# One rotation of banks for two passes, factors of the q weights loaded early, one border memset per pair of stages, and the relu of k ahead of the widening

## The chip, the cores and the metric

The kernel runs on one core of one Trainium2 chip. The metric is device time in microseconds (us), taken as the median over several executions. PE is the matrix engine (TensorE), DVE the vector engine, ACT the scalar engine, POOL is GpSimd and SP is the engine whose queue issues all of this kernel's DMAs. A time such as "1958.7" is a place on the time axis of the one profiled execution, counted from the start of its span.

## The reference

Two layers follow each other on x of shape (8, 256, 64, 64), in float32.

```
# layer 0: attention with reduced keys
xr  = layernorm_over_channels(conv(x, w_sr, stride 4))      # 16 x 16 places
q   = w_q x ;  k, v = split(w_kv xr)                         # 8 heads of 32
x   = x + gamma_s * w_out( softmax(q k^T / sqrt(32)) v )
# layer 1: linear attention at two scales
qkv = w_qkv x                                                # 768 channels
dw  = depthwise_conv_5x5(qkv, w_dw)
agg = grouped 1x1 conv of dw (w_pw, 96 groups of 8)
ms  = concat(qkv, agg)                                       # 64 heads of 8
q, k = relu(q), relu(k);  v = [v, 1]
out = q (k^T v);  out = out[:-1] / (out[-1] + 1e-15)
x   = x + batchnorm(w_proj out)
```

## The kernel before

The work is done in three passes over all images. The **first pass** (`first_pass`, 0 to about 1928 us) does layer 0 and the product by `w_qkv`. Its loop counts 128 steps `n`, one for half of a strip of an image. In a step PE makes scores (L849), their product with v (L881) and the output product (L949), and then some products of `qkv` (L996). `qkv` of an image's group `g` (four groups an image, so 32 in all) is made with seven products in place of eight for each of three pairs of outputs; DVE and ACT combine the seven from PSUM. The pairs are made in the order 1 (k), 2 (v), 0 (q). Pairs 0 and 1 go to DRAM scratch as planes with a border of zeros (`stage`, L1009), through two tiles `stage0` and `stage1` with one buffer each. The border is written by POOL with `memset`, in `new_stages` (L972), for each pair anew: pair 1 in step n+1, pair 0 in step n+3. Pairs 1 and 2 also go out as tokens through transposed tiles (`turned`, L1016). At the end of the pass two numbers that say whether the softmax sums stayed in bounds are reduced on DVE, summed with one matmul (`total`, L1195), and compared (L1197 to L1200).

The **second pass** (`second_pass`, about 1928 to 2966 us) loops over 64 units `u`, one for each (t, k, b): two halves t, four groups of channels k, eight images b. For one unit it loads the grids `d`, the tokens `kq` and `vq` (eight DMAs, `load_tokens` L1281), makes the depthwise and grouped convolution together as matmuls over widened weights `w` (L1389 in `convolve`, and L1420 in `product`, which does two units of q at once), the sums of k by v for the plain scale (`raw`, L1458) and for the convolved one (`sums`, L1483), and counts (L1470, ones by a sum over tokens of k that POOL makes: `red_raw` and `red_agg`, L1366 to L1368). DVE and POOL make differences of the grids first (`c`, L1310 and L1312, and `y`, L1338 and L1339). ACT takes the relu of the loaded k (`positive`, L1373) and of the convolved one (`r`). The weights are widened from small factors `wd` and `ws` (`factors`, L570), by ACT (L592, L615), DVE and POOL (L603); these are `chores`, of which `do(n)` takes the next n. A unit with image 1 or 2 is "wide": it takes 13 chores at the place where others take 4.

The **third pass** (about 2807, interleaved with the end of the second, to 3525 us) loads the kv sums (`kvp`, `kvq`, L1742 and L1744, summed by DVE at L1754 and L1755 and spread at L1758 and L1764), and per part of an image the denominators (`den`, L1816), their reciprocal, its spread over channels (`rep`, L1834), the product with q by DVE (L1839) and the projection (`p`, L1850).

Instructions are put in order on each engine by a scheduler with a cost model, except where `keep_in_program_order` (called `pinned` in the second pass) holds them in the order of the program text. The tile framework adds the waits. A tile pool's memory that is taken over by a later pool waits for the last readers of what was there before. Both passes make their own PSUM pools: the first rotates through eight banks with a list `turns`, the second has a pool each for `cv` (6 banks), `raw` and `sums` (1 each). So the first matmul of the second pass waits for all banks of the first:

```
psums = {
    tag: ctx.enter_context(tc.tile_pool(name=f"psum_{tag}", bufs=1, space=bass.MemoryType.PSUM))
    for tag in ("cv", "raw", "sums")
}
```

The end of a unit's step in the second pass, where the relu and the chores lie, is:

```
        products(u, 1)
        ...
        do(13 if wide else 4)
        if now:
            summed_raw(u)
        ...
        if u + 1 < n_all:
            positive(u + 1)
            reduced_raw(u + 1)
```

Of the kernel before, what the change touches and what calls it, by code (L numbers as in the profile page):

```python
# [32 lines left out]
P = 128  # L33
# [536 lines left out]
def factors(nc, home, a, j, k, n):  # L570


    wd = home.tile([P, 4, n, R * R], F32, tag=f"wd_{n}", name=f"wd_{j}_{k}")
    ws = home.tile([P, 4, D1], F32, tag=f"ws_{n}", name=f"ws_{j}_{k}")
    nc.sync.dma_start(wd[:, :, :4], a.w_big[:, j, 4 * k : 4 * k + 4].rearrange("p g (n f) -> p g n f", n=4))
    nc.sync.dma_start(ws, a.w_small[:, j, 4 * k : 4 * k + 4])
    across = wd[:, :, n - (2 if n == 6 else 3) :][:, :, :2]
    nc.vector.tensor_add(across, wd[:, :, 0:4:2], wd[:, :, 1:4:2])
    if n == 9:
        nc.vector.tensor_add(wd[:, :, 4], wd[:, :, 1], wd[:, :, 3])  # L580
        nc.vector.tensor_add(wd[:, :, 5], wd[:, :, 0], wd[:, :, 2])
        nc.vector.tensor_add(wd[:, :, 8], wd[:, :, 6], wd[:, :, 7])
    return wd, ws
# [45 lines left out]
def first_pass(ctx: ExitStack, tc: tile.TileContext, a, fine, planes, x2d, kd, vd, ready):  # L629
# [12 lines left out]
    psum = ctx.enter_context(tc.tile_pool(name="psum", bufs=1, space=bass.MemoryType.PSUM))  # L642
    turns, kept = list(range(8)), {}
# [12 lines left out]
    def load(src, name):  # L656
        consts[name] = const.tile(list(src.shape), F32, tag=name, name=name)
        nc.sync.dma_start(consts[name], src)
# [313 lines left out]
    def new_stages(b, g, pair):  # L972
        for j in (2 * pair, 2 * pair + 1):
            st = rest.tile([P, 4, NB + 1, NB + 1], F32, tag=f"stage{j % 2}", name=f"stage_{b}_{g}_{j}", bufs=1)
            tc.keep_in_program_order(nc.gpsimd.memset(st[:, :, 0 if g // 2 else NB], 0.0))
            tc.keep_in_program_order(nc.gpsimd.memset(st[:, :, :, 0 if g % 2 else NB], 0.0))
            staged[b, g, j] = st
# [3 lines left out]
    def qkv(b, g, pair):  # L981
# [5 lines left out]
        stages = [staged.pop((b, g, j)) for j in js] if pair < 2 else None  # L987
# [71 lines left out]
        def p1():  # L1059
            ps = product(1, w[:, 0, 0], b11)  # L1060
            u[1] = part(1)
            nc.scalar.copy(u[1], ps)  # L1062
# [28 lines left out]


# [33 lines left out]
    for n in range(n_all + 6):  # L1126
        now, was = n < n_all, 0 <= n - 1 < n_all
        at = n % 16
        filled = now and n // 16 + 1 < B
        if filled and at == 5 and n > 16:  # L1130
            load_x(n // 16 + 1)
        if filled and at == 5:
            ahead = keys_values(n // 16 + 1)
            next(ahead)
        if now and at == (10 if n < 16 else 1):
            border(n // 16)

        if now:
            e0 = scores(*order[n], 0, q[n])
            ej[n] = joined(*order[n], e0)  # L1140
        if (n, 0) in blank:
            new_stages(*blank.pop((n, 0)), 0)
        catch_up(late)
        if was:
            p = order[n - 1]
            for kc in range(2):
                valued(*p, kc, es[n - 1][kc])
            counted(*p, ej.pop(n - 1))
            es.pop(n - 1)
            copied(*p)  # L1150
            normed(*p)
        if now:
            es[n] = e0, scores(*order[n], 1, q.pop(n))
            joined_too(ej[n], es[n][1])
        catch_up(later)
        if (n, 1) in blank:
            new_stages(*blank.pop((n, 1)), 1)

        products = todo.pop(n, [])
        taps = 2 if filled and 6 <= at < 10 else 0  # L1160
        for f in products[:3]:
            f()
        if filled and at >= 10:
            next(ahead, None)
        for _ in range(taps):
            next(ahead)
        if 0 < n + 1 < n_all:
            if n + 1 not in q:
                q[n + 1] = queries(*order[n + 1])
        for f in products[3:]:  # L1170
            f()
        if was and p[2]:
            b, s = p[:2]
            pair = [att[b, s, 0], att[b, s, 1]]
            for oc in range(2):
                added(b, s, pair, oc)
            if s % 2:
                differences(b, s // 2)
                blank[n + 1, 1] = blank[n + 3, 0] = b, s // 2
                rest_of = [f for pair in (1, 2, 0) for f in qkv_lazy(b, s // 2, pair)]  # L1180
                for i, count in enumerate((7, 4, 7, 3)):
                    todo[n + 1 + i] = rest_of[:count]
                    rest_of = rest_of[count:]
        for _ in range(taps):
            next(ahead)
        if filled and at >= 10:
            next(ahead, None)
        if now and n >= n_all - 40:
            next(ready, None)


    both = halves.tile([P, 2], F32, tag="both", name="both")
    nc.vector.tensor_reduce(both, seen.rearrange("p (n k) -> p k n", k=2), AX.X, ALU.add)
    total = bank("total")[:, :2]
    nc.tensor.matmul(total, mean_w, both, start=True, stop=True)  # L1195
    fits = halves.tile([P, 4], F32, tag="fits", name="fits")
    nc.vector.tensor_scalar(fits[:, 0:1], total[:, 0:1], SUM_MAX / D0 / C, None, ALU.is_le)  # L1197
    nc.vector.tensor_scalar(fits[:, 1:2], total[:, 1:2], INVERSE_MAX / D0 / C, None, ALU.is_le)
    nc.vector.tensor_mul(fits[:, 2:3], fits[:, 0:1], fits[:, 1:2])
    nc.vector.tensor_copy(fine, fits[:, 2:3])  # L1200

# [8 lines left out]
def second_pass(ctx: ExitStack, tc: tile.TileContext, a, planes, kd, vd, kept, first_w, kvd, kvg, qd, ahead):  # L1215
    nc = tc.nc
    B = a.x.shape[0]
    def pool(name, bufs=1):
# [4 lines left out]
    late, quads, between, const, small, third, w_q = (  # L1223
        pool("late2"), pool("quads2"), pool("between2", 2), pool("const2"), pool("small2", 2), pool("third2"),
        pool("wq2"),
    )
    soon = ExitStack()
    second, even, first, odd, extra, w_taps, pairs, sides, mid = (
        soon.enter_context(tc.tile_pool(name=name, bufs=bufs))
        for name, bufs in (  # L1230
            ("second2", 1), ("even2", 1), ("first2", 1), ("odd2", 1), ("extra2", 1), ("taps2", 1), ("pairs2", 1), ("sides2", 2),
# [3 lines left out]
    psums = {  # L1235
        tag: ctx.enter_context(tc.tile_pool(name=f"psum_{tag}", bufs=1, space=bass.MemoryType.PSUM))
        for tag in ("cv", "raw", "sums")
    }

    pinned = tc.keep_in_program_order  # L1240

    def bank(tag, name, bufs=1, n=512):
        return psums[tag].tile([P, n], F32, tag=tag, name=name, bufs=bufs)

    units = [(t, k, b) for t in range(2) for k in range(4) for b in range(B)]
# [57 lines left out]
    def paired(u, i):  # L1303
        d = grids[u]
        c = cells[u, i] = pairs.tile([P, 4, (NB + 1) * NB // 2], F32, tag=f"c1_{i}", name=f"c1_{u}_{i}")
        v = c.rearrange("p g (y x) -> p g y x", x=NB // 2)
        d0, d1, d2 = (d[:, :, :, i : i + NB - 1 : 2] for i in range(3))
        if i == 2:

            pinned(nc.gpsimd.tensor_copy(v, d1))  # L1310
        else:
            nc.vector.tensor_sub(v, d2 if i else d0, d1)  # L1312
# [68 lines left out]
    def convolve(u, i):  # L1381
        t, k, b = units[u]
        c, w = cells[u, i], wt[t, k]
        ps = bank("cv", f"cv1_{u}_{i}", 6)
        for g in range(4):
            for da in range(2):
                n = 2 * da + i if i < 2 else 4 + da
                cols = slice(da * (NB // 2), da * (NB // 2) + P)
                nc.tensor.matmul(  # L1389
# [6 lines left out]
        if i == 2:  # L1396
            both = between.tile([P, QB], F32, tag="both", name=f"both1_{u}")
            nc.scalar.copy(both, ps)
            r = (second if u % 2 else sides).tile([P, 2, 4, P], F32, tag="r1", name=f"r1_{u}", bufs=1)
# [9 lines left out]
    def product(m, i, j):  # L1409
        t, k, b = units[2 * m]  # L1410
        now, w = quad[m], wq[t, k, (i, j)]
        ps = bank("cv", f"cv0_{m}_{i}{j}", 6)
        for g in range(4):
# [6 lines left out]
            nc.tensor.matmul(out, w[:, g], x, start=True, stop=True)  # L1420
# [31 lines left out]
    def summed_raw(u):  # L1452
        kq, vq = kqs.pop(u), vqs[u]
        ps = bank("raw", f"raw_{u}")
        for i in range(8):
            r, c = i // 4, i % 4
            for f in range(4):
                nc.tensor.matmul(  # L1458
# [8 lines left out]
    def counted(ps, at, red):  # L1467
        for j in range(4):
            cols = slice(j * D0, (j + 1) * D0)
            nc.tensor.matmul(ps[cols, at : at + 1], red[:, cols], ones, start=True, stop=True)  # L1470
# [5 lines left out]
    def summed(u):  # L1476
# [3 lines left out]
        for i in range(8):  # L1480
            par, r, c = i // 4, i // 2 % 2, i % 2
            for h in range(4):
                nc.tensor.matmul(  # L1483
# [23 lines left out]
    def ended_raw(u):  # L1507
# [3 lines left out]
        mraws[u] = m  # L1511

# [34 lines left out]
    def load_factors(u, what):  # L1547
        t, k, b = units[u]
        j = t + 2 * what
        parts[j, k] = factors(nc, kept if what else w_q, a, j, k, 6 if what else 9)  # L1550

    def spare(name):
        return bank("cv", name, 6)

    load_factors(0, 0)
# [3 lines left out]
    reduced_raw(0)  # L1559
    for u in range(n_all + 3):  # L1560
# [21 lines left out]
        if u < 2:  # L1582
            chores.append(weights_q(0, u))
# [14 lines left out]
        do(3 if wide else 2)  # L1598
# [7 lines left out]
        do(3 if wide else 2)  # L1606
# [8 lines left out]
        if u in (n_all - 1, n_all + 1):  # L1615
            ahead.send(spare)
        do(13 if wide else 4)
# [8 lines left out]
        if u + 1 < n_all:  # L1626
            positive(u + 1)
# [28 lines left out]
def third_pass(ctx: ExitStack, tc: tile.TileContext, a, planes, x2d, kvd, kvg, qd, out, kept, top):  # L1656
# [119 lines left out]
    def folded(b, get=None):  # L1776
        dw, kt = folds[b]
        wp = homes["mid"].tile([P, 4, C], F32, tag="wp", name=f"wp_{b}") if b else first_wp
# [216 lines left out]
def kernel_body(ctx: ExitStack, tc: tile.TileContext, a, out):  # L1995
# [22 lines left out]
    with ExitStack() as held:  # L2018
        kept = held.enter_context(tc.tile_pool(name="kept", bufs=1))
        first_w = kept.tile([P, 4, 6 * P], F32, tag="w1_0", name="w1_0_0")  # L2020

        def ready():
            yield from widened_k(tc, first_w, *factors(nc, kept, a, 2, 0, 6))

        first_pass(tc, a, fine, planes, x2d, kd, vd, ready())
        top = held.enter_context(tc.tile_pool(name="top3", bufs=1, side="right"))
        ahead = third_pass(held, tc, a, planes, x2d, kvd, kvg, qd, out, kept, top)
        second_pass(tc, a, planes, kd, vd, kept, first_w, kvd, kvg, qd, ahead)
# [125 lines left out]
```

## Time and profile before

| | us |
|---|---|
| median of 3 runs (from, to) | 3544.17 (3543.93, 3544.29) |
| the profiled execution, its time | 3526.67 |
| its span | 3524.9 |
| PE busy | 3449.2 (98%) |
| DVE busy | 2251.0 (64%) |
| POOL busy | 1844.9 (52%) |
| ACT busy | 1473.7 (42%) |

The span is the time from the first to the last instruction that the profiler saw; the execution's own time is 1.8 us longer. The mean granted clock of PE is 0.99 of full speed. A line of a timeline shows the start, the duration, the engine, the line of the code, the operation with what it writes and reads, how many of them lie together, and, in brackets, the idle time ahead of it on its engine with the instruction or transfer that ended it. In the list of waits a line shows who waited for whom: in all, how often, and the longest.

### The profile page before, as it was taken

Reading aid. Unit: us, or ns where it says so; the run is one execution under the profiler, and the core shown is the slowest. Engines: PE = TensorE matmul, PEld = TensorE weight load, DVE = VectorE, ACT = ScalarE, POOL = GpSimd, SP = SyncE. Lnnn points to the kernel's source line nnn. Section 1 sums busy time; section 2 is a strip of 40 time slices with the busy share of each in tenths; the row PEclk is TensorE's granted clock in tenths of the full one; section 3 lists DMA queues with packets and bytes.
Section 4 is the critical chain, followed back from the end, with each engine's and each line's share of the span. In section 5 each row is a group of like instructions: output and inputs, shape, how many; then the busy total and the mean of one; then the engine's idle time right before and its main releaser. Section 6 shows DMA issues by size and latency. Waiting matters only on the chain.

```text
span 3524.9 us, 92777 instructions
## 1 busy us (share of the span) xinstructions
PE 3449.2 (98%) x38818; PEld 2105.2 (60%) x38818; DVE 2251.0 (64%) x3441; ACT 1473.7 (42%) x3385; POOL 1844.9 (52%) x1756
## 2 busy tenths in 40 slices
PE   8999999999999999999999899999999999999998
PEld 5554555555546555455444788888888874333343
DVE  1567476576675765766777677777777774544443
ACT  2345354353453544544553444444444332333332
POOL 3557466465564664655664555666656642222221
PEclk9999999999999999999999999999999998999999
DMA  5445446355364463553555999999999978787872
GB/s 175 115 108 159 122 112 173 96 163 147 89 172 118 102 188 93 148 154 92 141 134 149 268 262 272 266 268 269 274 268 266 274 209 253 232 237 228 242 220 88
DMA packets 577196, 647.36 MB, mean 184 GB/s; under 512 B 81664, under 2 KB 452864, under 8 KB 576768
## 3 DMA queue, kind: packets, MB, share of 16 engines
q1 hardware_dynamic: 576768, 641.34, 65.0%
q8 instruction: 307, 5.03, 0.6%
q14 instruction: 121, 0.99, 0.1%
HBM read 389.85 MB, written 249.23 MB: 181 GB/s over the span
## 4 chain that ended last, share of the span: by engine, by line
PE 90%; DMA 4%; SPq 2%; ACT 1%; POOL 1%; DVE 1%; issue 1%; DVEq 0%; POOLq 0%; ACTq 0%
PE qkv L996 17%; PE p L1850 11%; PE cv L1389 9%; PE sc L849 8%; PE av L881 7%; PE cv L1420 7%; PE sums L1483 6%; PE o L949 6%; PE q L831 6%; PE sr L752 6%; PE av L907 2%; PE rep L1834 2%; PE den L1816 1%; PE raw L1458 1%; DMA raw<-planes 1%
## 5 line engine op out<-in xcount | busy, mean ns | idle before, releaser
L862 ACT ACTIVATE e<-sc 128x512 f32<-128x512 f32 x1024 | 528.6, 603 | 508.4 <-PE sc L849 508.4
L901 POOL TENSOR_TENSOR ef<-ef,e 128x512 f32<-128x512 f32 x512 | 688.3, 1354 | 91.1 <-ACT e L862 67.5
L894 POOL TENSOR_TENSOR ef<-e 128x512 f32<-128x512 f32 x256 | 329.6, 1307 | 545.8 <-ACT e L862 545.7
L1389 PE MATMUL cv<-w,c 128*128 128x128 f32 x3072 | 386.5, 280 | 5.9 <-DVE stage L1009 4.2
L1860 POOL TENSOR_TENSOR y<-z,xs 128x512 f32<-128x512 f32 x120 | 156.1, 1303 | 445.5 <-ACT z L1858 382.2
L1389 PEld LDWEIGHTS cv<-w,c 128*128 128x128 f32 x3072 | 363.4, 194 | 7.7 <-POOL c L1310 4.7
L849 PE MATMUL sc<-q,kk 32*64 32x256 f32 x8192 | 298.5, 387 | 5.6 <-ACT e L862 5.2
L996 PE MATMUL qkv<-differences,combined 128*128 128x512 f32 x576 | 289.2, 593 | 0.4 <-POOL differences L966 0.4
L928 DVE STREAM_TRANSPOSE rden<-av 128x256 f32<-128x256 f32 x256 | 99.7, 427 | 283.6 <-ACT att L919 236.1
L1483 PE MATMUL sums<-vq,r 128*32 128x288 f32 x4096 | 265.6, 407 | 0.2
L1858 ACT ACTIVATE z<-p,held 128x512 f32<-128x512 f32 x128 | 99.5, 777 | 374.6 <-PE p L1850 368.5
L849 PEld LDWEIGHTS sc<-q,kk 32*64 32x64 f32 x8192 | 155.3, 131 | 163.0 <-issue 101.4
L881 PE MATMUL av<-e,vv 64*32 64x256 f32 x8192 | 252.3, 379 | 0.0
L752 PE MATMUL sr<-x,wsr 128*128 128x256 f32 x1024 | 236.1, 383 | 8.0 <-DMA wsr<-in_w_sr_dram 7.7
L831 PE MATMUL q<-x,wq 128*128 128x512 f32 x512 | 241.9, 594 | 0.0
L1366 POOL TENSOR_TENSOR red_raw<-kq 128x512 f32<-128x512 f32 x64 | 82.1, 1282 | 298.7 <-ACT kq L1373 239.7
L752 PEld LDWEIGHTS sr<-x,wsr 128*128 128x128 f32 x1024 | 194.8, 191 | 64.5 <-issue 31.6
L949 PE MATMUL o<-att,wout 128*128 128x512 f32 x512 | 230.3, 592 | 0.0
L934 DVE TENSOR_TENSOR att<-att,rall 128x512 f32<-128x512 f32 x128 | 217.3, 1698 | 4.4
L1850 PE MATMUL p<-raw,wp 128*128 128x512 f32 x448 | 215.7, 603 | 1.8 <-ACT wp L1785 1.8
L1012 DVE TENSOR_TENSOR whole<-part,qkv 128x512 f32<-128x512 f32 x256 | 172.2, 682 | 66.6 <-ACT part L1062 49.4
L1420 PE MATMUL cv<-y,w 128*128 128x128 f32 x1536 | 200.6, 277 | 10.2 <-POOL y L1339 7.2
(174 smaller groups left out, 6058.8 us busy)
## 6 DMA issues: line engine op xcount, KB each, us to landing
planes<-stage SPq DMA_DIRECT2D x128, 578.0 KB
d<-planes SPq DMA_DIRECT2D x128, 578.0 KB
vq<-v SPq DMA_DIRECT2D x256, 256.0 KB
raw<-planes SPq DMA_DIRECT2D x64, 578.0 KB
x<-in_xp_dram SPq DMA_DIRECT2D x64, 512.0 KB
wsr<-in_w_sr_dram SPq DMA_DIRECT2D x128, 256.0 KB
x<-x SPq DMA_DIRECT2D x128, 256.0 KB
k<-turned SPq DMA_DIRECT2D x256, 128.0 KB
```

What stands on the lines that cost most here:

```text
L752: nc.tensor.matmul(ps[:, oc], w[:, ci, oc * P : (oc + 1) * P], strips(b, f // 2)[:, ci, f % 2 * NK : (f % 2 + 1) * NK], start=(f == ci == ...
L831: nc.tensor.matmul(ps, consts["wq"][:, ci, c * P : (c + 1) * P], strips(b, s)[:, ci], start=(ci == 0), stop=(ci == 1),)
L849: nc.tensor.matmul(scs[h][HALVES[half], QH[kq % 2]], kks[b][rows, c, kq * P // 2 : (kq + 1) * P // 2], qs[rows, QH[half]], start=True, sto ...
L862: nc.scalar.activation(e[:, h % 2].rearrange("p q n -> p (q n)"), scs[h], AF.Exp, scale=D0**-0.5)
L881: nc.tensor.matmul(sums["av"][half][cols, : QB // 2], vvs[b][rows, kq, c * P + h * D0 : c * P + (h + 1) * D0], es[h // 2][rows, h % 2, kq ...
L901: tc.keep_in_program_order(nc.gpsimd.tensor_tensor(f, f, e[:, :, half], ALU.add))
L949: nc.tensor.matmul(ps, consts["wout"][:, c, oc * P : (oc + 1) * P], att[c], start=(c == 0), stop=(c == 1))
L996: nc.tensor.matmul(ps, w, x, start=True, stop=True)
L1389: nc.tensor.matmul(ps[:, g * P : (g + 1) * P], c[:, g, cols], w[:, g, n * P : (n + 1) * P], start=(da == 0), stop=(da == 1),)
L1420: nc.tensor.matmul(out, w[:, g], x, start=True, stop=True)
L1483: nc.tensor.matmul(ps[h * D0 : (h + 1) * D0, : 36 * D1].rearrange("p (r n e) -> p r n e", r=3, e=D1), kt[:, par, h, 2 * r + c], vq[:, r : ...
L1850: nc.tensor.matmul(as_block(ps, i // 2), wp[:, i, oc * P : (oc + 1) * P], block(g, i // 2, i % 2, j), start=(i == 0), stop=(i == 3),)
```

## The change

The change has these parts.

1. One PSUM pool with eight banks serves both passes; the second pass takes bank 2 for `raw`, bank 6 for `sums` and the others for `cv`. The matmuls of the second pass are pinned until the raw sums of three units are through.
2. The factors of the first q weights (`wd`, `ws`, with nine sets each) are loaded in the first pass, into the memory of the weights for k and v (`wkv`), and summed there. 18 of the q weights' chores are done ahead of unit 0, and units' first two `do` are empty for u = 0. The scheduler also puts vq_0's eight loads into the first pass.
3. `new_stages` is called once for both pairs, in step n+1.
4. `positive(u + 1)` comes ahead of `do(13 if wide else 4)`.
5. `total` and the comparisons move into step n_all + 2 of the first pass. For units 0 and 1 the copy of c_2 is ACT's in place of POOL's.
6. Some tiles change pools: `const2`, `r1` of odd units, and `wp` of odd images. With this the scheduler issues the kvp and kvq loads of images 1 and 2 ahead of the loads of raw and agg where the third pass begins, and puts DVE's sums of them among the last instructions of the second pass.

```
 def factors(nc, home, a, j, k, n):
-    wd = home.tile([P, 4, n, R * R], F32, tag=f"wd_{n}", name=f"wd_{j}_{k}")
-    ws = home.tile([P, 4, D1], F32, tag=f"ws_{n}", name=f"ws_{j}_{k}")
+    if n == 9:
+        t = home.tile([P, 2 * 2 * C], F32, tag="wkv", name=f"wd_{j}_{k}")
+        wd = t[:, : 4 * n * R * R].rearrange("p (g n f) -> p g n f", g=4, n=n)
+        ws = t[:, 4 * n * R * R : 4 * (n * R * R + D1)].rearrange("p (g o) -> p g o", g=4)
+    else:
+        wd = home.tile([P, 4, n, R * R], F32, tag=f"wd_{n}", name=f"wd_{j}_{k}")
+        ws = home.tile([P, 4, D1], F32, tag=f"ws_{n}", name=f"ws_{j}_{k}")
     nc.sync.dma_start(wd[:, :, :4], ...)
     nc.sync.dma_start(ws, a.w_small[:, j, 4 * k : 4 * k + 4])
+    return wd, ws
+
+def summed_factors(nc, wd):
+    n = wd.shape[2]
     across = wd[:, :, n - (2 if n == 6 else 3) :][:, :, :2]
     nc.vector.tensor_add(across, wd[:, :, 0:4:2], wd[:, :, 1:4:2])
     if n == 9:
         ...
-    return wd, ws

 def first_pass(...):
-    psum = ctx.enter_context(tc.tile_pool(name="psum", bufs=1, space=bass.MemoryType.PSUM))
-    turns, kept = list(range(8)), {}
+    kept = {}
...
-    def new_stages(b, g, pair):
-        for j in (2 * pair, 2 * pair + 1):
-            st = rest.tile([P, 4, NB + 1, NB + 1], F32, tag=f"stage{j % 2}", name=f"stage_{b}_{g}_{j}", bufs=1)
+    def new_stages(b, g):
+        for j in range(2):
+            st = rest.tile([P, 4, NB + 1, NB + 1], F32, tag=f"stage{j}", name=f"stage_{b}_{g}_{j}", bufs=1)
...
-        if (n, 0) in blank:
-            new_stages(*blank.pop((n, 0)), 0)
         catch_up(late)
+        if n == n_all + 2:
+            bounded()
...
         catch_up(later)
-        if (n, 1) in blank:
-            new_stages(*blank.pop((n, 1)), 1)
+        if n in blank:
+            new_stages(*blank.pop(n))
...
-                blank[n + 1, 1] = blank[n + 3, 0] = b, s // 2
+                blank[n + 1] = b, s // 2

 def second_pass(...):
-    psums = {
-        tag: ctx.enter_context(tc.tile_pool(name=f"psum_{tag}", bufs=1, space=bass.MemoryType.PSUM))
-        for tag in ("cv", "raw", "sums")
-    }
-    def bank(tag, name, bufs=1, n=512):
-        return psums[tag].tile([P, n], F32, tag=tag, name=name, bufs=bufs)
+    turns = {"cv": [turns[i] for i in (0, 1, 3, 4, 5, 7)], "raw": [turns[2]], "sums": [turns[6]]}
+    def bank(tag, name):
+        i = turns[tag].pop(0)
+        turns[tag].append(i)
+        return psum.tile([P, 512], F32, tag=f"bank{i}", name=name)
+    def multiply(*args, **flags):
+        made = nc.tensor.matmul(*args, **flags)
+        if len(begun) < 3:
+            pinned(made)
...
-        if i == 2:
+        if i == 2 and u < 2:
+            nc.scalar.copy(v, d1)
+        elif i == 2:
             pinned(nc.gpsimd.tensor_copy(v, d1))
...
-            r = (second if u % 2 else sides).tile([P, 2, 4, P], F32, tag="r1", name=f"r1_{u}", bufs=1)
+            r = (extra if u % 2 else sides).tile([P, 2, 4, P], F32, tag="r1", name=f"r1_{u}", bufs=1)
...
-    load_factors(0, 0)
+    parts[0, 0] = first_parts
     for i in (2, 0, 1):
         paired(0, i)
     positive(0)
     reduced_raw(0)
+    chores.append(weights_q(0, 0))
+    do(18)
...
-        if u < 2:
-            chores.append(weights_q(0, u))
+        if u == 1:
+            chores.append(weights_q(0, 1))
...
-        do(3 if wide else 2)
+        do(0 if not u else 3 if wide else 2)
...
-        do(3 if wide else 2)
+        do(0 if not u else 3 if wide else 2)
...
         products(u, 1)
+        if u + 1 < n_all:
+            positive(u + 1)
         do(13 if wide else 4)
...
         if u + 1 < n_all:
-            positive(u + 1)
             reduced_raw(u + 1)

 # third pass, folded(b)
-        wp = homes["mid"].tile([P, 4, C], F32, tag="wp", name=f"wp_{b}") if b else first_wp
+        if b % 2:
+            wp = kept.tile([P, 2 * 2 * C], F32, tag="wkv", name=f"wp_{b}").rearrange("p (j n) -> p j n", j=4)
+        else:
+            wp = homes["mid"].tile([P, 4, C], F32, tag="wp", name=f"wp_{b}", bufs=1) if b else first_wp

 # kernel_body
+            wd, ws = factors(nc, kept, a, 2, 0, 6)
+            summed_factors(nc, wd)
+            yield from widened_k(tc, first_w, wd, ws)
+            first_parts.extend(factors(nc, kept, a, 0, 0, 9))
+            yield
+            summed_factors(nc, first_parts[0])
+        banks = ExitStack()
+        psum = banks.enter_context(tc.tile_pool(name="psum", bufs=1, space=bass.MemoryType.PSUM))
+        turns = list(range(8))
```

`bounded()` is a new function that holds the lines L1192 to L1200 of before unchanged.

## The prediction

> **What bounds the kernel now.** First the page's head and its chain of work, to see which engine sets the end:
>
> ```profile
> span 3524.9 us, 92777 instructions
> PE 3449.2 (98%) x38818; PEld 2105.2 (60%) x38818; DVE 2251.0 (64%) x3441; ACT 1473.7 (42%) x3385; POOL 1844.9 (52%) x1756
> PE 90%; DMA 4%; SPq 2%; ACT 1%; POOL 1%; DVE 1%; issue 1%; DVEq 0%; POOLq 0%; ACTq 0%
> ```
>
> PE works 98% of the span, so only the other 76 us, and matmuls at a lowered clock, can be won: the change takes no matmul away. Next the timeline of PE where the first pass gives way to the second (start, duration, what ran, idle time ahead of it and who ended it):
>
> ```profile
> 1923.59 0.38 PE L1195 MATMUL total<-both,mean_w 128*128 128x2 f32 x2 [1.90 <-DVE whole L1012]
> 1928.22 12.36 PE L1389 MATMUL cv<-w,c 128*128 128x128 f32 x96 [4.24 <-DVE stage L1009]
> ...
> 1952.86 1.08 PE L1458 MATMUL raw<-vq,kq 128*32 128x32 f32 x64 [6.08 <-ACT kq L1373]
> 1955.60 0.29 PE L1470 MATMUL raw<-ones,red_raw 128*32 128x1 f32 x8 [1.66 <-POOL red_raw L1368]
> 1958.16 0.29 PE L1470 MATMUL sums<-ones,red_agg 128*32 128x1 f32 x8 [2.27 <-POOL red_agg L1368]
> 1958.79 3.51 PE L1389 MATMUL cv<-w,c 128*128 128x128 f32 x16 [0.35 <-POOL c L1310]
> ```
>
> and the same stretch by windows (from:to, length, busy us and instructions of PE, PE's weight loads, DVE, ACT, POOL; granted clock; DMA share; GB/s):
>
> ```profile
> 1928.20:1933.50 5.30, 5.28 (x35) 5.30 (x36) 0.03 (x1) 0.00 (x0) 2.78 (x4) 0.72 0.79 147
> ...
> 1946.80:1958.70 11.90, 1.65 (x80) 1.35 (x80) 4.55 (x10) 9.88 (x34) 7.01 (x8) 0.70 1.07 298
> 1958.70:1962.30 3.60, 3.51 (x21) 3.39 (x24) 3.31 (x7) 0.00 (x0) 3.52 (x4) 0.56 1.08 356
> ```
>
> From 1921.6 to 1983.0 (61.4 us) PE does what takes 37.3 us at its later pace: 176 matmuls of L1389 by 0.112 us, 64 of L1420 by 0.112, 192 of L1458 in 2.1, 128 of L1483 in 8.0, 0.3 for the counts. So 24.1 us are lost here: about 17 idle, about 7 at clocks of 0.56 to 0.72. The waits of PE from 2010 to 2800 name one more thing, y, and the timeline of one such place shows why:
>
> ```profile
> PE cv L1420 <- POOL y L1339: 7.2, 6, 2.2
> ```
>
> ```profile
> 2193.87 2.95 ACT L615 ACTIVATE w<-wd,ws 128x64 f32<-128x64 f32 x12
> 2196.72 1.04 ACT L1373 ACTIVATE kq<-kq 128x1024 f32<-128x1024 f32 x1
> 2197.84 1.28 POOL L1366 TENSOR_TENSOR red_raw<-kq 128x512 f32<-128x512 f32 x1 [10.58 <-ACT kq L1373]
> 2201.22 1.53 POOL L1339 TENSOR_TENSOR y<-d 128x512 f32<-128x512 f32 x1
> ```
>
> ACT widens 12 weights, then does the relu; POOL, idle for 10.58 us, starts red_raw only then, and y stands behind red_raw. Last, where the third pass begins:
>
> ```profile
> 2942.96 0.30 DVE L1754 TENSOR_TENSOR kvp<-kvp 128x132 f32<-128x132 f32 x1 [11.97 <-DMA kvp<-kv]
> 2945.39 2.47 DVE L1839 TENSOR_TENSOR agg<-agg,rep 128x512 f32<-128x512 f32 x4
> 2946.13 9.56 PE L1834 MATMUL rep<-rec,rep_w 32*128 32x512 f32 x24 [5.78 <-DVE agg L1839]
> ```
>
> DVE, in order, stands before a small sum (kvp) whose load is late; the product that frees PE's bank is behind it.
>
> **The change, part by part.** Sums are made within the profiled execution: span 3524.9, itself 3526.67, 17.5 us under the median of runs (3544.17); I carry the difference over unscaled.
>
> *Handover, start.* With one rotation of banks the first cv waits for its own bank and for c_2, now copied by ACT (about 0.7 us, as POOL's copy takes 0.70), no longer for the last stage write: 4.24 are given back, and 1.90 by `total`, which moves two steps back and takes 0.57 us of small DVE operations along. Against it: on DVE, which is busy 35.8 of the last 41.6 us of the pass, two widenings of q weights (2.28 us as at 1947.82) and their four sums (0.95) come in ahead, and three c subtractions (0.71 each) stand before the last stage writes. The last transposed v is done about 1.9 us later than 1922.9. Sixteen v stores (8.6 us of SP) follow it, then the two stage stores; before, these landed at 1937.8. I put T = 1939.8.
>
> *Handover, the gate.* T still matters: the tiles of both1_0 on ACT and of eps on DVE reuse memory that these stores read, as before (ACT's copy began at 1938.0, DVE's eps at 1938.1). Queued behind them: on ACT the second copy, r, and the relu of k for unit 1; on DVE every s, the tap sums, c_2. PE waits for all of these. Five groups of 16 cv (9 us) and raw_0 run before T; then PE is idle. From T: two copies and r on ACT 2.2; the relu, no longer behind 34 ACT instructions (9.88 us), done at T+3.3; raw_1 there (1943, before 1952.86); sums_0 to T+8.5, with red_raw and red_agg on POOL (3.3 and 2.5) beside it; counts, cv_1_1, cv_2_2; the tap sums of DVE (1.9) and c_2_1 at T+11.9 = 1951.7.
>
> *Handover, the transfers.* The next product needs d0. vq_0's eight loads (1.5 MB) and the factors were put hundreds of us earlier, where DMA is half idle, so ten issues fewer stand ahead. From 1933.5 SP sends 5.7 MB up to d0 (sizes from the page's list of DMA issues). Here a rule is to be weighed. The trace moved 7.4 MB from 1931.7 to 1960.5: 257 GB/s. The Trainium skill ("DMA: Bandwidth & Descriptors", "Anatomy of one DMA") fits about 2.0 us plus bytes over 436 GB/s, for another issue path. By the row d0 lands at 1933.5 + 22.2 = 1955.7; by the rule at 1948.6, before anyone asks. I take the row, since its mix of transfers is the same. Then y for it 2.3 us, the rest of the stage 11.3 us, and a restart of the clock: after 6.1 us of idleness the first 32 cv took 5.23 us instead of 3.58, so 1.7. The stage's mark (unit 3's first cv, 1975.5 before) comes at 1971: **4.5 us gained**. By the rule the gate is c_2_1: near 1965, 10 gained. If only T's delay worked, -2; all of the loss recovered, 24.
>
> *Relu ahead.* In the six places the relu passes 4 to 13 widenings (1 to 3 us), more than each wait (at most 2.2). The widenings come 1.04 later; their weights are for the next group of units. What could turn it round is k landing late, for ACT would stop with r and the weights behind it: in every unit to 2780 k had landed 19 us or more before its relu. **6 of 7.2 gained** (3 to 7).
>
> *Third pass.* The kvp and kvq loads of two images are issued ahead of raw and agg, in SP's idle time after 2876.8; the first waits for an earlier product, half of them stand behind a store of q that waits for ACT's r (2879.4 before). So DVE isn't stopped at 2943: 5.8, and 1.5 from the den matmuls behind it (3.36 instead of 1.9). Their sums (two sets: about 4.8 us by the rows of 0.18 to 0.30) now stand in DVE's tail from 2889 to 2904.7, where DVE has no gap and PE's p waits for it: 4.8 lost. Raw and agg are issued some 1.2 us later there, covered by 20 us of p. **2.5 gained** (7 gained to 5 lost: a kv load landing late in the tail stops DVE at once).
>
> *At nothing.* The 128 memsets fewer (0.16 to 0.22 us each) lie in POOL's idle time; the one that stays waits, as before, for the preceding group's store at the same step. Factors and vq_0 in the first pass: 10 issues of 0.6 us on SP, which waits for DVE and PE for hundreds of us there. First-pass PE order is untouched but for `total`. Tiles that change pools (const2, r1, wp of odd images) keep their number of buffers.
>
> Sum: 4.5 + 6 + 2.5 = 13. Span 3511.9; median 3544.17 - 13 = **3531.2**.
>
> **Rivals.** *The handover is recovered wholly* (the stores land early, d0 in time): 24 + 6 + 2.5 = 32, 3512; halfway to it, 3521. For it: raw_1's gate of 10 us goes; against: d0 is at the end of a full DMA queue (share 1.07 in the window).
> *Hidden by the transfers*: the second pass keeps DMA at 266 to 274 GB/s and 0.92; a PE that is 10 us ahead only meets the loads, and gains of the first two parts melt. Against: PE waits for no transfer between 2010 and 2800. If so, 0 + 2 + 2.5: 3540, or no change.
> *Slower, by the border*: with one memset for two pairs, pair 0's first write into the stage waits on DVE itself for pair 1's store; attention's products are queued behind it. Price 32 groups times the wait; it makes the kernel slower from (13 + 7.1)/32 = 0.63 us each; at 1.0, 3563. Before, POOL met this wait once (5.2 us), and DVE, which had it too, never.
>
> **How the numbers follow.** A measurement can tell 0.2% (7.1 us) here. The likeliest, some 7 to 20 us gained: 0.62, 3524 to 3537. Wholly or nearly recovered: 0.13, down to 3512. Swallowed, within 7.1: 0.14. Slower: 0.11, from 3552. So faster 0.75, same 0.14, slower 0.11. The range 3520 to 3544 leaves out some 0.08 below and 0.12 above.
>
> **What would show it.** First cv within 1 us of the last qkv, no wait for stage; raw of unit 1 near 1943; the next idle time of PE ended by d (DMA) or c; unit 3's first cv near 1971. No PE wait for POOL y above 0.5 us from 2010 to 2800. No DVE wait for kvp at 2943, p waiting for side 5 us or more at 2905. Wrong it is if the stage stores land after 1945, if DVE waits for planes<-stage in the first pass, or if ACT waits for k's load.

## The result and the profile after

| | before | after |
|---|---|---|
| median of the runs taken side by side, us | 3542.16 (8 runs) | 3526.23 (8 runs) |
| ratio, 95% interval | 1 | 0.9957 (0.9946 to 0.9967) |
| the profiled execution, its time | 3526.67 | 3526.32 |
| its span | 3524.9 | 3524.5 |

The changed kernel is 0.43% faster: 15.2 us on 3544.17, where 13 were forecast. The two *profiled* executions, however, are equally long. Single executions of one kernel scatter by some 3 to 6 us (standard deviation), and the profiled one of before was shorter than all eight timed runs of it in this set. So the traces are compared by stages here, and several executions of each kind were taken. The page of the changed kernel begins:

```profile
span 3524.5 us, 92769 instructions
...
PE 3452.9 (98%) x38818; PEld 2104.6 (60%) x38818; DVE 2265.3 (64%) x3441; ACT 1476.4 (42%) x3387; POOL 1821.6 (52%) x1626
```

The matmuls are as many as before, and POOL has 130 instructions fewer. PE is still the bound. The timeline of PE at the handover (same columns as before: start, duration, what ran, idle time ahead and who ended it) shows what happened there. The last product of the first pass began at 1926.18 here and at 1920.67 before, so times are also counted from there.

```profile
1928.05 2.05 PE L1251 MATMUL cv<-w,c 128*128 128x128 f32 x16 [0.85 <-ACT c L1320]
1930.94 2.05 PE L1251 MATMUL cv<-w,c 128*128 128x128 f32 x16 [0.84 <-DVE c L1324]
...
1936.46 0.99 PE L1251 MATMUL raw<-vq,kq 128*32 128x32 f32 x61 [3.47 <-issue]
...
1946.72 1.06 PE L1251 MATMUL raw<-vq,kq 128*32 128x32 f32 x64 [2.42 <-ACT kq L1385]
...
1957.21 1.35 PE L1251 MATMUL cv<-w,c 128*128 128x128 f32 x10 [0.41 <-DVE c L1324]
1959.24 1.29 PE L1251 MATMUL cv<-d,w 128*128 128x128 f32 x8 [0.68 <-DMA d<-planes]
1962.50 1.16 PE L1251 MATMUL cv<-y,w 128*128 128x128 f32 x8 [1.06 <-DVE y L1350]
...
1971.71 1.95 PE L1251 MATMUL cv<-w,c 128*128 128x128 f32 x16
```

(All matmuls of the second pass carry line L1251 now, that of the helper which pins them.) The wait of 4.24 for the stage is gone, and that for the relu of k has shrunk from 6.08 to 2.42. What is left are pieces of 0.4 to 3.5, of which the longest (3.47, "issue") has no cause that the profile shows, and PE comes to d 0.68 us before the transfer has landed. Unit 3's first cv, the mark of the prediction, stands 45.5 us after the last product of the first pass (1971.71), before it was 54.8: 9.3 us gained in this stage. The windows of the same stretch (from:to, length, busy us and instructions of PE, PE's weight loads, DVE, ACT, POOL; granted clock; DMA share; GB/s):

```profile
1926.20:1936.40 10.20, 5.11 (x35) 3.90 (x33) 9.20 (x14) 6.09 (x19) 4.20 (x4) 1.00 0.85 193
1936.40:1946.70 10.30, 7.83 (x120) 7.65 (x120) 3.52 (x7) 3.08 (x7) 0.00 (x0) 0.83 0.94 277
1946.70:1958.70 12.00, 11.43 (x186) 8.38 (x186) 4.89 (x9) 6.70 (x19) 10.11 (x11) 0.86 1.08 307
1958.70:1962.50 3.80, 2.19 (x17) 2.03 (x17) 3.30 (x3) 0.59 (x1) 3.06 (x2) 1.00 1.08 309
```

Before, PE was busy 1.65 of 11.9 us in the window ahead of c, with ACT full of widenings; now 11.43 of 12. The clock is 0.83 to 1.00, where three windows before had 0.56 to 0.72. DMA is as full as it was.

In the second pass, the waits of PE from 2010 to 2800 (who waited for whom: us in total, times, longest) have a new first line:

```profile
PE cv L1251 <- ACT w L624: 4.2, 6, 1.4
PE cv L1251 <- POOL y L1351: 2.0, 2, 1.1
```

y was 7.2 in 6 waits; it is 2.0 now, and 4.2 of waits for widened weights w have come. One such place in the timeline:

```profile
2655.09 1.05 ACT L1385 ACTIVATE kq<-kq 128x1024 f32<-128x1024 f32 x1
2656.03 2.98 ACT L624 ACTIVATE w<-wd 128x64 f32<-128x64 f32 x12
2656.22 1.28 POOL L1378 TENSOR_TENSOR red_raw<-kq 128x512 f32<-128x512 f32 x1 [8.69 <-ACT kq L1385]
2659.05 1.06 PE L1251 MATMUL cv<-d,w 128*128 128x128 f32 x6 [1.18 <-ACT w L624]
```

ACT does the relu (1.05 us) first, POOL has its sum early, and the last of 12 widenings comes 1.05 us later: just what the next matmul reads.

In the third pass the stop of DVE at 2943 is gone, but there is one like it 30 us on (timeline; SPq is SP's queue, with the times of its transfers' issue):

```profile
2944.26 20.66 SPq L1973 DMA_DIRECT2D out_dram<-y  x2
2964.96 3.10 SPq L1759 DMA_DIRECT2D kvp<-kv  x1
...
2973.12 0.30 DVE L1771 TENSOR_TENSOR kvp<-kvp 128x132 f32<-128x132 f32 x1 [12.66 <-DMA kvp<-kv]
2973.59 1.28 DVE L1859 TENSOR_TENSOR agg<-agg,rep 128x512 f32<-128x512 f32 x2
2974.33 3.26 PE L1854 MATMUL rep<-rec,rep_w 32*128 32x512 f32 x5 [3.92 <-DVE agg L1859]
```

Two output stores, the second of which waits for its y, hold SP for 20.66 us; the kv loads of image 3 stand behind them, DVE stands 12.66 us before image 3's sum, and PE waits 3.92 us for the product behind that sum, and then runs at half clock.

### The profile page after: what moved, and what is told of

It reads as the page before. It is cut to its first block, busy times and chain, and to the rows that moved or that the text cites. A ratio compares the mean times of both kernels' runs of the same rounds, so it can differ in the third digit from the quotient of the medians.

```text
span 3524.5 us, 92769 instructions
## 1 busy us (share of the span) xinstructions
PE 3452.9 (98%) x38818; PEld 2104.6 (60%) x38818; DVE 2265.3 (64%) x3441; ACT 1476.4 (42%) x3387; POOL 1821.6 (52%) x1626
## 4 chain that ended last, share of the span: by engine, by line
PE 88%; DMA 5%; DVE 2%; ACT 2%; SPq 1%; POOL 1%; issue 1%; DVEq 0%; ACTq 0%; POOLq 0%
PE qkv L1004 17%; PE cv L1251 13%; PE p L1870 12%; PE sc L857 8%; PE av L889 7%; PE sr L760 6%; PE o L957 6%; PE q L839 6%; PE sums L1251 6%; DMA d<-planes 2%; PE rep L1854 2%; PE av L915 2%; PE den L1836 1%; PE raw L1251 1%; DMA vq<-v 1%; DMA raw<-planes 1%
## 5 line engine op out<-in xcount | busy, mean ns | idle before, releaser
L1251 PE MATMUL cv<-w,c 128*128 128x128 f32 x3072 | 383.4, 278 | 2.1 <-DVE c L1324 1.3
L1251 PEld LDWEIGHTS cv<-w,c 128*128 128x128 f32 x3072 | 360.4, 193 | 4.3 <-ACT c L1320 1.7
L1251 PE MATMUL sums<-vq,r 128*32 128x288 f32 x4096 | 264.4, 408 | 0.0
L1870 PE MATMUL p<-agg,wp 128*128 128x512 f32 x448 | 210.4, 592 | 0.0
```

The lines of the kernel that those rows point to most:

```text
L1251: made = nc.tensor.matmul(*args, **flags)
L1870: nc.tensor.matmul(as_block(ps, i // 2), wp[:, i, oc * P : (oc + 1) * P], block(g, i // 2, i % 2, j), start=(i == 0), stop=(i == 3),)
```

## The experiments

The stages of all profiled executions, in us (length; in brackets, PE idle and the time at half clock by the trace's record of the granted clock). "Handover" runs from the start of the very last first-pass matmul (0.43 us after the row of two that is counted from above) to the second group of cv over d; "second pass" from there to the 28th such group; "third" from the 32nd and last of them to the first p over the later images' weights (wp). The other stages agree within a few us: between the 28th and the 32nd group lie 127.6 to 131.7 us, and the start, whose code is the same in all, ends at 77 to 84, with 6.8 to 17.1 us of it at half clock.

| kernel | first pass | handover | second pass | third |
|---|---|---|---|---|
| before | 1843.6 | 70.9 (17.2, 17.1) | 759.1 | 124.7 |
| before again | 1843.6 | 70.8 (17.1, 17.1) | 762.5 | 124.6 |
| border alone | 1843.6 | 72.6 (17.4, 20.5) | 769.0 | 125.4 |
| relu alone | 1849.4 | 69.4 (15.1, 17.1) | 756.8 | 125.5 |
| memory alone | 1846.0 | 62.9 (8.8, 13.7) | 763.4 | 126.8 |
| after | 1843.8 | 61.6 (9.7, 6.8) | 756.9 | 129.7 |
| after again | 1843.8 | 61.7 (9.8, 6.8) | 764.3 | 129.8 |
| after, two rotations | 1842.1 | 62.8 (11.6, 10.2) | 760.2 | 128.3 |
| after, relu late | 1842.1 | 61.6 (9.3, 6.8) | 765.9 | 127.6 |
| after, relu earlier | 1848.9 | 61.6 (9.2, 6.8) | 754.6 | 126.8 |
| after, sums late | 1848.9 | 61.7 (9.2, 6.8) | 763.0 | 119.6 |
| both of these | 1848.9 | 61.7 (9.3, 6.8) | 755.1 | 117.3 |

**The kernels as they are, again.** Nothing is edited.

> The kernel before, unchanged, as a second look at it: its profiled execution (3526.67 us) lay below all of its eight timed ones (3534.6 to 3546.1), so one trace of it is not its usual run. Ratio 1.000 within 0.2%. If the missing 8 to 19 us are a property of the usual run, this trace shows them at one place (start of the first pass, handover, second pass or third pass); if they are made of many small ones, no stage differs by more than 3 us from the first trace.

> The changed kernel once more, on the same chip as the next three. By its first runs 0.9957 of before; by the stages of the first trace 9.3 us less at the handover, about 3 less in the second pass, 5 more where the third pass begins: 7 to 8 us in all, 0.998. If the ratio comes again near 0.996 and the trace shows the same stages, the other 7 us lie in spans that differ from execution to execution (the start, single windows of half clock). If 0.998, the first ratio was partly chance.

Before again: 0.9996 (0.9984 to 1.0007) of before. After again: 0.9957 (0.9943 to 0.9970), in a second set of runs. The gain stands. The table shows what repeats: the handover within 0.1 us, the third pass within 0.1. The second pass does not: 759.1 and 762.5 for before, 756.9 and 764.3 for after. One execution can't settle a question of 4 us there.

**The relu alone**, in the kernel before:

```
+        if u + 1 < n_all:
+            positive(u + 1)
         do(13 if wide else 4)
...
         if u + 1 < n_all:
-            positive(u + 1)
             reduced_raw(u + 1)
```

> Before, with nothing changed but the place of the relu of k (ahead of the widening). The prediction's term: 6 us of the 7.2 us of waits for y from 2010 to 2800 go, and at the handover the relu of unit 1 is no longer behind the widening, so up to 6 us there: 3530 to 3536 against 3542. Rival (the second pass is held by the transfers): waits for y go, other waits come, the time stays within 2 us of before.

Measured: 0.9971 (0.9962 to 0.9981), 10 us faster. PE's waits for y are gone from 2010 to 2800, and there are some for w:

```profile
PE cv L1420 <- ACT w L615: 3.8, 5, 1.4
```

At the handover it moved the relu and won only 1.4 us (69.4). The timeline of PE says who is late next:

```profile
1940.23 12.41 PE L1389 MATMUL cv<-w,c 128*128 128x128 f32 x96 [4.22 <-POOL c L1310]
...
1965.15 0.29 PE L1470 MATMUL raw<-ones,red_raw 128*32 128x1 f32 x8 [4.67 <-POOL red_raw L1368]
1968.08 0.29 PE L1470 MATMUL sums<-ones,red_agg 128*32 128x1 f32 x8 [2.64 <-POOL red_agg L1368]
```

The wait of 4 us at the start is there still, and that for the relu has become one for the counts of k.

**The relu late**, in the kernel after: the same edit backwards.

```
-        if u + 1 < n_all:
-            positive(u + 1)
         do(13 if wide else 4)
...
         if u + 1 < n_all:
+            positive(u + 1)
             reduced_raw(u + 1)
```

> The changed kernel with the relu of k back behind the widening, everything else as changed. Four traces with the old place have 759 to 769 us (mean 763.5) in the second pass and 7 to 13 us of waits for y; five with the new place 757 to 764 (mean 760) with 6 to 9 us of waits for weights and y. So by the traces the relu is worth 3 to 4 us of the second pass in the changed kernel: 3530 to 3533, ratio 0.997. Done alone in before it was worth 10 us by the timed runs; if that holds here, 3537, ratio 0.9985. The handover grows by at most 2 us, since the weights no longer stand ahead of unit 1's relu in the queue.

Measured: 0.9965 (0.9951 to 0.9980), against 0.9957 of after: about 3 us slower than after, and the intervals overlap. PE's waits from 2010 to 2800 are those of before, somewhat longer:

```profile
PE cv L1251 <- POOL y L1351: 11.4, 9, 2.2
PE cv L1251 <- ACT w L624: 1.4, 1, 1.4
```

The handover is 61.6 without the moved relu too. So it plays no part there once the memory is changed.

**The memory alone**: the kernel before with the q weights' factors in the memory of `wkv`, and pools moved as in the change; rotations, relu and border as before.

```
+    if n == 9:
+        t = home.tile([P, 2 * 2 * C], F32, tag="wkv", name=f"wd_{j}_{k}")
...
-        parts[j, k] = factors(nc, kept if what else w_q, a, j, k, 6 if what else 9)
+        parts[j, k] = factors(nc, kept, a, j, k, 6 if what else 9)
...
-            r = (second if u % 2 else sides).tile([P, 2, 4, P], F32, tag="r1", name=f"r1_{u}", bufs=1)
+            r = (extra if u % 2 else sides).tile([P, 2, 4, P], F32, tag="r1", name=f"r1_{u}", bufs=1)
```

With it the scheduler again puts vq_0's eight loads and those of the first q weights' factors far into the first pass (1726 to 1743, and 1671).

> Before, with the memory of the changed kernel alone (factors of q and wp of odd images in the slot of the k and v weights, const and r moved), which gives the changed kernel's order of kvp and kvq loads at the start of the third pass; factors still loaded in the second pass. The prediction's term: 2.5 us faster (7 faster to 5 slower). By the trace of the changed kernel, where the stop of DVE before kvp is gone at 2943 and comes again for the next image at 2973, with 3.9 us of idle PE and 6.8 us more at half clock: 0 to 5 us slower.

Measured: 0.9967 (0.9954 to 0.9979). The handover is 62.9: 8.0 of the 9.3 us come with this part, though PE starts the second pass 8.6 us after the last product, later than before (7.6):

```profile
1929.56 0.38 PE L1200 MATMUL total<-both,mean_w 128*128 128x2 f32 x2 [1.91 <-DVE whole L1017]
1935.20 6.40 PE L1393 MATMUL cv<-w,c 128*128 128x128 f32 x32 [5.25 <-DMA v<-turned]
...
1942.26 7.41 PE L1393 MATMUL cv<-w,c 128*128 128x128 f32 x64
```

From 1935.20 PE runs on without the 6 us gap behind the first 96 cv. The timeline of ACT points to one of the loads. Before, ACT stands 5.62 us until DVE has summed the factors of the q weights (wd, whose load is issued only at 1941.39), then widens 17 weights, and the relu of unit 1's k comes behind them:

```profile
1947.66 4.20 ACT L615 ACTIVATE w<-wd,ws 128x80 f32<-128x80 f32 x17 [5.62 <-DVE wd L580]
```

With the factors there since the first pass, the widening starts without a wait:

```profile
1945.26 1.06 ACT L620 ACTIVATE w<-wd 128x64 f32<-128x64 f32 x4
```

The raw sums of unit 1 follow 24.5 us after the last product instead of 32.2. That it is the factors, and not vq_0 or another of the moved tiles, was not tested apart. The third pass isn't shorter: 126.8.

**Two rotations of banks**, in the kernel after: the pool is closed between the passes and made anew.

```
         first_pass(tc, a, fine, planes, x2d, kd, vd, ready(), psum, turns, kept)
+        banks.close()
+        psum = banks.enter_context(tc.tile_pool(name="psum2", bufs=1, space=bass.MemoryType.PSUM))
```

> The changed kernel, with the second pass on a PSUM pool of its own again, so that its first product waits for all banks of the first pass; everything else as changed. If the handover's length is set by the landing of the stage stores and of d0 (the prediction's gate), unit 3's first cv comes within 2 us of the changed kernel's, and the time is 3526 to 3529. If the sharing of banks carries the gain: 3.5 to 6 us slower than the changed kernel, 3530 to 3533.

Measured: 0.9953 (0.9939 to 0.9967), as after. The timeline of PE at the handover:

```profile
1929.52 6.61 PE L1251 MATMUL cv<-w,c 128*128 128x128 f32 x32 [7.94 <-issue]
...
1943.27 0.73 PE L1251 MATMUL raw<-vq,kq 128*32 128x32 f32 x62 [0.86 <-ACT kq L1385]
...
1954.87 1.30 PE L1251 MATMUL cv<-d,w 128*128 128x128 f32 x8 [0.73 <-DMA d<-planes]
```

Without shared banks PE stands 7.94 us at the start and waits 1.6 us less at the relu, and meets d with the same 0.7 us to spare. The stage is 1.2 us longer. One rotation for both passes, the part named first in the title, is worth about 1 us: what PE does early there it waits for later.

**The border alone**, in the kernel before:

```
-                blank[n + 1, 1] = blank[n + 3, 0] = b, s // 2
+                blank[n + 1] = b, s // 2
...
-        if (n, 0) in blank:
-            new_stages(*blank.pop((n, 0)), 0)
...
-        if (n, 1) in blank:
-            new_stages(*blank.pop((n, 1)), 1)
+        if n in blank:
+            new_stages(*blank.pop(n))
```

> Before, with one border memset for both pairs of stages and nothing else. The prediction: nothing, within 2 us of before, first pass 1843.6 us between the first output product and the last qkv as before. Rival of the prediction (pair 0's first write waits for pair 1's store on DVE): 0.6 us or more in each of 32 groups, 20 us slower.

Measured: 0.9999 (0.9990 to 1.0008), and 1843.6 in the first pass as before. It is worth nothing that can be told, in either direction (the interval is 3 us wide to each side).

**The relu earlier**, in the kernel after: ACT has an idle gap of about 1.7 us ahead of the r of `products`; the relu fits in it and then delays no weight.

```
+        if u + 1 < n_all:
+            positive(u + 1)
         products(u, 1)
...
-        if u + 1 < n_all:
-            positive(u + 1)
         do(13 if wide else 4)
```

> The changed kernel with the relu of k one place earlier still, ahead of the r of the q units, where ACT waits 1.7 us for DVE before that r in a wide unit. In the changed kernel's trace PE no longer waits for y 7.2 us from 2010 to 2800 but 2.0, and now waits 4.2 us for the last widened weights, which the relu made 1.04 us late. If that is what the relu costs, both waits go here: 4 to 6 us less than the changed kernel in the second pass. If r is made late instead, PE waits for sums or counts and the time stays.

Measured: 0.9967 (0.9955 to 0.9979), no better than after. The second pass, 754.6, is the shortest of all, but w is still waited for 3.7 us in 4 waits, so the gap covers only a part.

**The sums late**, in the kernel after: from image 3 on the sums of kvp and kvq, and DVE's products with q, are held in the order of the text (of each sum its first addition, the one that waits for the load), so that no product stands behind a sum whose load is late.

```
-            nc.vector.tensor_add(kv[:, :, :2], kv[:, :, :2], kv[:, :, 2:])
+            made = nc.vector.tensor_add(kv[:, :, :2], kv[:, :, :2], kv[:, :, 2:])
+            if b >= 3:
+                tc.keep_in_program_order(made)
...
-            nc.vector.tensor_mul(q, q, as_block(banks[j], s))
+            made = nc.vector.tensor_mul(q, q, as_block(banks[j], s))
+            if not get:
+                tc.keep_in_program_order(made)
```

> The changed kernel, with DVE's products by the spread reciprocals and its sums of kv (from image 3 on) held in program order, so that DVE doesn't stand before kvp of image 3 at 2973. If that stop is what the start of the third pass lost: PE's 3.9 us there and some 7 us at half clock go, the stage from the last q product of the second pass to the first regular p is 125 us or less (129.7 changed, 124.7 before), 5 to 8 us off the time. Rival (the loads set the pace there): DVE then waits for agg or raw at about the same time, and the stage keeps its 128 to 130 us.

Measured: 0.9930 (0.9916 to 0.9943), wholly below the interval of after. Third is 119.6, 10 us less than after and 5 less than before. DVE's timeline in this kernel:

```profile
2973.63 2.48 DVE L1861 TENSOR_TENSOR agg<-agg,rep 128x512 f32<-128x512 f32 x4 [2.53 <-PE rep L1856]
2981.76 2.48 DVE L1861 TENSOR_TENSOR agg<-agg,rep 128x512 f32<-128x512 f32 x4 [5.66 <-PE rep L1856]
```

DVE waits for PE's rep now, not PE for DVE: of the whole stretch from 2885 to 3010 the waits of rep for agg are

```profile
PE rep L1856 <- DVE agg L1861: 0.8, 1, 0.8
```

against 4.7 in 2 waits in the kernel after.

**Both**, the relu earlier and the sums late:

> The changed kernel with both mends: the sums of kv of later images held behind the products on DVE, and the relu ahead of the q units' r. The first gave 10 us at the start of the third pass. If the second is worth nothing (0.9967 against 0.9957 beside it), the ratio is 0.993 again; if it takes the remaining 6 us of waits for weights and y, 0.9915.

Measured: 3509.52 us (3508.18 to 3515.44), 0.9918 (0.9900 to 0.9936). It beats both kernels; against the sums late alone (0.9930) the intervals overlap, so that the earlier relu pays is not shown.

## Why the prediction was right, and where its steps were not

The sign and the size held, and the handover is the largest gain in the traces. The sum of 13 us is nevertheless made of three terms of which none has its measured size: 4.8 too little at the handover, 2 to 3 too much for the relu, 7.6 too much in the third pass. By the traces' stages the change would be worth 8, so that the sum comes within 2 us of the timed 15 is in part luck.

**Handover: 4.5 forecast, 9.3 measured.** The course was right: first cv early, raw_1 gated by the relu, then d by its transfer. Counted from the last product, the forecast has the transfers up to d0 start at 12.8 us, d0 land at 35.0 and the mark at 50.3; the trace has 10.1, 32.9 (1959.11) and 45.5. So two stretches were mis-sized.

*The start of the transfers* was put 2.8 us too late. The rows of SP's queue, before and after:

```profile
1922.99 8.60 SPq L1046 DMA_DIRECT2D v<-turned  x16
1931.70 1.16 SPq L1030 DMA_DIRECT2D planes<-stage  x2
```

```profile
1928.64 7.50 SPq L1054 DMA_DIRECT2D v<-turned  x16
1936.24 1.27 SPq L1038 DMA_DIRECT2D planes<-stage  x2
```

DVE's extra work was to make the last transposed v 1.9 us later, but its stores start 2.5 us after the last product, before 2.3, and the sixteen of them take 7.5 us instead of 8.6. *T*, the landing of the last stage stores, was put too late with it: it is 17.3 us after the last product (1943.52), before 17.1, forecast 19.1. The transfers from there to d0 were weighed rightly: 22.9 us, where 22.2 were forecast. They are 5770 KB by the profile's list of DMA issues, or 5.9 MB, so 258 GB/s (the forecast's 5.7 and 7.4 MB take a KB as 1000 bytes, which cancels in its sum). The rate in the Trainium skill ("DMA: Bandwidth & Descriptors", "Anatomy of one DMA": 2.0 us and bytes over 436 GB/s) would, as an estimate, have landed d some 7 us earlier; here the measurement decides against it.

*From d's landing to the mark* it took 12.6 us, where 15.3 were put. Of these 1.7 are *the restart of the clock*, which did not come: from 1958.70 on the granted clock is 1.00. For 1.0 I have no cause. The steps account for the difference: 2.8 - 0.7 + 2.7 = 4.8.

What brings the gain was less well seen: the prediction put the relu's 6 us first and the early transfers beside it, and did not name ACT's 5.62 us before the factors at all. The runs show the moved memory, with the early loads that come with it (8.0 alone), to do nearly all of it, one rotation 1 us, and the moved relu none once they are there. Alone it brings 1.4.

**Relu: 6 forecast.** y's waits fall, as said: 7 to 13 us in the five kernels with the relu behind the widenings, 0 to 2 in those with the relu just ahead of them (two waits of up to 1.1 us stay in the kernel after, where none above 0.5 was forecast). The step that failed is "The widenings come 1.04 later; their weights are for the next group of units": the last widenings of a unit are read by the very next group of matmuls, and waits for w grow from 0 to 2 us to 4 to 7. By the table, the five old places average 764.0 in the second pass and the five new ones with the relu just ahead of the widenings (relu alone, after twice, two rotations, sums late) 760.2: about 4 us, with a scatter of 3 to 4 us in each five, so that the waits show the effect better than the lengths. Timed, it is 3 in company (0.9965 to 0.9957, overlapping) and 10 alone. The first of these is uncertain by some 6 us and the second by 3 to 4, so it is not shown that the relu is worth less beside the others.

**Third pass: 2.5 gained forecast, 5.1 lost in both traces.** The step "So DVE isn't stopped at 2943" is right word for word, and wrong in what it stands for. The forecast followed the loads of two images. The third image's loads are behind two waiting stores, and its sum stops DVE just the same, 30 us later and with less cover. The forecast's extra sums in the tail did cost little (PE's p waited 2.57, before 2.36, not 5). The loss is larger than PE's 3.9 us of waiting: PE is idle as long as before (8.9 and 9.4 us), but at half clock for 30.7 us instead of 23.9, of which half, 3.4, is lost. That names some 3 of the 5; about 2 stay open, with the same matmuls in the stage. Four other kernels with this order of loads (memory alone, two rotations, relu late and relu earlier) take 126.8 to 128.3 us there, so they lose 2 to 4. The kernel with the sums late shows the stop to be the cause: it takes PE's wait there away, and third falls by 10 us, 4.8 of them in less idle time (4.1) and 5 in less half clock (20.5).

**At nothing** was right: the border alone is at 0.9999, and the first pass keeps its length. Where it differs by 5 us (1848.9 against 1843.8), the code is the same and the half clock is 13.7 us instead of 3.4: half of 10.3 is 5.2.

**The rivals.** Slower by the border falls by its own run. Hidden by the transfers falls: in the kernel after PE waits for no transfer from 2010 to 2800. Wholly recovered has 9.3 of its 24.

**What stays open.** By stages the traces give about 9 at the handover, 4 in the second pass and 5 lost in the third, so 8; the timed runs give 15. The parts that were timed are the memory alone, 12, and the relu in company, 3. The second pass alone spreads by some 4 us from one execution to the next. The mean granted clock of the timed runs is about 0.989 for before and 0.991 for after, and 0.990 and 0.991 in their first traces: 0.002 of 3530 us are 7 us, half of which the traces don't show. So a part of the rest may lie in clock windows, whose number in a single execution is in part chance (see the last section); which part of the change makes them fewer, and where the remainder lies, was not settled. Relu alone 10 and memory alone 12 make 22, where together they make 15; the intervals of the three are 3 to 5 us to each side, so this gap of 7 is about as large as their noise.

## What to carry to other kernels

When a stop of an in-order engine before a late load is taken away, follow the same load for every later round of the loop: here the first image's stop went and the third's came, and holding products ahead of sums gained 10 us at the start of the third pass, where the changed kernel had lost 5. A wait priced at zero because "that result is for later" has to be checked against who reads the last of the delayed results, since a shift of 1 us meets the reader that has the least slack. And the name of a change is no guide to its parts: of the gain at the handover, the shared banks made 1 us and the moved memory, with its early loads, 8.

## What was not expected of the hardware

The lowered clock comes in windows of 3.4 us or multiples of it (3.4, 6.8, 10.2, 13.7, 17.1, 20.5; only the last of each trace, which its end cuts off, is of another length). That length agrees with the Trainium skill ("TensorE: Matmul & The Clock Gate", "Part 1: The HAM clock gate"), which ties half clock to a window of idleness. But in these traces much less idleness goes before it. In the first pass PE is idle for only 6.6 to 7.1 of some 1845 us, and seven times in each trace it waits 0.74 us for `e` from ACT. Of these 84 waits in twelve traces 23 are followed by a window at half clock, none to four in a trace, and the first pass has no others.

Which of the waits these are can be read from the times. In each trace all windows at half clock start at whole multiples of 3.413 us from each other. Laid on that grid, the 23 waits begin 0.02 to 0.64 us after a step of it, and the other 61 at 0.65 us or more. Here are two waits of the kernel before, at 0.09 and at 2.95 us, and the next step of the grid after the start of each (columns as above; the clock is the third number from the end):

```profile
648.59 2.06 PE L849 MATMUL sc<-q,kk 32*64 32x256 f32 x28 [0.74 <-ACT e L862]
886.96 2.06 PE L849 MATMUL sc<-q,kk 32*64 32x256 f32 x28 [0.74 <-ACT e L862]
```

```profile
651.17:654.58 3.41, 3.41 (x6) 1.35 (x5) 2.82 (x4) 1.73 (x4) 3.33 (x4) 0.50 0.00 0
886.69:890.11 3.42, 3.15 (x31) 1.58 (x32) 1.43 (x4) 3.42 (x11) 2.64 (x3) 1.00 0.24 68
```

So in these traces the same short wait cost 1.7 us or nothing, by where it fell on the grid, and that differs between executions of the same code: the changed kernel's first pass took 1842.1 us with no such window and 1848.9 with four. That is a scatter of up to 6.8 us which no edit of the first pass causes. Why the first 0.64 us of a step matter was not tested.
